# Graph net, second layer: a block's outputs turned in squares by VectorE and through DRAM instead of by TensorE

## Chip, core and metric

One core of one Trainium2 chip runs the whole program in one launch. The metric is the device time in microseconds (us); the time before is the median of three runs. The engines are TensorE (PE in the profile, its weight loads PEld), VectorE (DVE), ScalarE (ACT), GpSimd (POOL) and SyncE (SP, which only issues transfers).

## The reference

Four graph layers on 4096 nodes with 256 features each, every one followed by a residual addition and a normalisation of the rows. All values are FP32. The change lies in the second layer, which is attention with four heads of 64 features, masked by the edges:

```python
def _L1_gnn_ref(x, edge, Wq, bq, Wk, bk, Wv, bv):
    q = _split_heads(x @ Wq + bq)
    k = _split_heads(x @ Wk + bk)
    v = _split_heads(x @ Wv + bv)
    mask = (edge.T.astype(jnp.float32) - 1.0) * 10000.0
    scores = jnp.einsum('hnd,hmd->hnm', q, k) / np.sqrt(HEAD_DIM)
    scores = scores + mask[None, :, :]
    attn = jax.nn.softmax(scores, axis=-1)
    ctx = jnp.einsum('hnm,hmd->hnd', attn, v)
    return ctx.transpose(1, 0, 2).reshape(x.shape[0], NHEAD * HEAD_DIM)
...
x = _layernorm(x + _L1_gnn_ref(x, adj, ...), axis=-1)
```

The first layer is a graph attention with leaky ReLU, the third one with a single head, and the fourth a cosine attention.

## The kernel before

The second layer's main stage works on eight blocks of 512 query rows (`NB`, `b`). A block has 64 steps (`NH`, `j`), one for each 64 keys. A step of a block does the following for all four heads at once, with keys on the partitions and query rows along the free axis:

- `scores` (line 861): eight products on TensorE into a PSUM tile `p` of two banks (L876), and the exponential in place on ScalarE (L878). Every fourth step asks SyncE for the next mask (L869).
- `weights` (line 880): VectorE multiplies by the mask out of PSUM into the SBUF tile `prob` (L888). The sums over the keys are kept in `den`: at even steps GpSimd adds `prob` to it (L898), at odd steps a transfer issued by GpSimd accumulates it (L904). At steps 44, 48, 52 and 56 (`relief`), in all blocks but the first, the even addition is put off and done by VectorE (L1005).
- `sums` (line 906): eight products on TensorE that add the weighted values to the PSUM tiles `acc0` and `acc1` (L912). They run three steps (`LAG`) behind the scores.

The tile `p` has three buffers, `prob` has eight, `acc` one. So the scores of a step need the buffer that VectorE read three steps ago.

At a block's last step the two `acc` tiles, which hold the outputs with features on the partitions and rows along the free axis, are copied to SBUF: `kept0` by ScalarE (L917) and `kept1` by VectorE (L918). The rest of the block, `finish(b, j)` (line 974), is spread over the steps of the next block. Its step `j` is issued in iteration `j + 3` of that next block, as the last thing of the iteration. It joins the key sums (`join_sums`, L921), adds them over the partitions on TensorE and copies them (`row_sums`, L934, L937), turns them on TensorE (`turned_row_sums`, L942), takes reciprocals, turns the outputs on TensorE (`turned_half`, four 128x128 turns for two groups of 128 rows, L949), scales each half in PSUM by the reciprocals (L963), adds it to the rows `X` (L966), and normalises the rows: `one_row` (statistics), `begin_root` (VectorE and ScalarE), `end_root` and `lift_mean` (six small operations on GpSimd, L168 to L191) and `scale_row` (VectorE, L186). The turned pieces take a buffer of `p` through `halves`.

The order on TensorE, VectorE and ScalarE is the order in which the code is written (`manual_schedule`); SyncE and GpSimd get theirs from the scheduler, by the due time of each instruction. The last block has no next block; its `tail` runs beside the third layer's start.

The fourth layer already turns its outputs in another way: VectorE transposes 32x32 squares (L1206), SyncE puts the quarters of the tile to a DRAM tile `away` (L1210) and fetches them back in the right order (L1213).

Of the kernel before, what the change touches and what calls it, by code (L numbers as in the profile page):

```python
# [9 lines left out]
FP = mybir.dt.float32  # L10
# [8 lines left out]
P = 128  # L19
D = 256  # L20
KC = D // P
QB = 4
QW = QB * P
# [5 lines left out]
def kernel(  # L29
# [92 lines left out]
    def turning_apart(squares, far, part, to, eng, between=False):  # L122

        B = P // QB
        squares = squares.tile([P, QB, KC, P], FP, name="squares")
        for c in range(KC):
            if c and between:
                yield
            nc.vector.transpose(squares[:, :, c, :].rearrange("p q (k n) -> p k q n", n=B),
                                part(c).rearrange("p k (q f) -> p k q f", f=B))  # L130
        yield
        far = far.tile([QB, B, QB, KC * P], FP, name="far")
        eng.dma_start(far.rearrange("a f q m -> (a f) (q m)"), squares.rearrange("p q c m -> p (q c m)"))
        yield
        to = to()
        for q in range(QB):
            eng.dma_start(to[q * B:(q + 1) * B], far[:, :, q, :].rearrange("a f m -> f a m"))
        return to.rearrange("p a (c m) -> p c a m", c=KC)

    def block_turning(sb, once, dr, rows, eng):  # L140
        to = lambda: sb.tile([P, KC * QW], FP, name="xT").rearrange("p (a m) -> p a m", a=QB)
        return turning_apart(once, dr, lambda c: rows[:, :, c * P:(c + 1) * P], to, eng)

    def at_once(steps):
        while True:
# [596 lines left out]
    def multi_head_attention(w_sb, b_sb, tail, rows_of_den, rows_done, narrow_edges, ga):  # L742
# [8 lines left out]
        MJ = 4  # L751
        NH = N // d
        W = KC * QW
        kept, den, rden, mvs, roots = {}, {}, {}, {}, {}
        with ExitStack() as lay:
            keep = pool(lay, "mh_keep", 1)
            kT = keep.tile([P, KC, N], FP, name="kT")
            qT = keep.tile([P, KC, N], FP, name="qT")
            V = keep.tile([P, NH, P], FP, name="V")
# [146 lines left out]
            def sums(b, j):  # L906
                if j == 0:
                    acc[b] = [pa.tile([P, QW], FP, name=f"acc{c}") for c in range(KC)]
                for r in range(KC):
                    for c in range(KC):  # L910
                        half = slice(c * d, (c + 1) * d)
                        nc.tensor.matmul(acc[b][c][r * d:(r + 1) * d, :], V[half, j, r * d:(r + 1) * d],  # L912
                                         prob[b, j][half, r, :], start=(j == 0), stop=(j == NH - 1))
                if j == NH - 1:

                    kept[b] = [fin1.tile([P, QW], FP, name=f"kept{c}") for c in range(KC)]
                    nc.scalar.copy(kept[b][0], acc[b][0])  # L917
                    (nc.scalar.copy if b == NB - 1 else nc.vector.tensor_copy)(kept[b][1], acc[b][1])  # L918

            def join_sums(b, n, eng=nc.vector):  # L920
                eng.tensor_tensor(den[b][:, 0, :], den[b][:, 0, :], den[b][:, n, :], OP.add)  # L921
# [1 line left out]
            def row_sums(bank, b):  # L923


                kept[b].append(fin1.tile([P, QW], FP, name=f"kept{KC}"))
                pds = [bank() for _ in range(KC)]
                for r in range(KC):
                    for s in range(2):
                        for c in range(KC):  # L930
                            g = 2 * r + s
                            half = slice(c * d, (c + 1) * d)
                            lo = r * QW + s * QW // 2
                            nc.tensor.matmul(pds[c][g * G:(g + 1) * G, :QW // 2], ones[half, :G],  # L934
                                             den[b][half, 0, lo:lo + QW // 2], start=True, stop=True)
                for c in range(KC):
                    nc.scalar.copy(kept[b][KC][:, c * QW // 2:(c + 1) * QW // 2], pds[c][:, :QW // 2])  # L937

            def turned_row_sums(bank, b):
                pd = bank()  # L940
                for k in range(QB):
                    nc.tensor.transpose(pd[:, k * P:(k + 1) * P], kept[b][KC][:, k * P:(k + 1) * P], ident)  # L942
                return pd

            def turned_half(bank, b, k):
                po = bank().rearrange("p (k f) -> p k f", f=D)
                for i in range(2):
                    for c in range(KC):
                        nc.tensor.transpose(po[:, i, c * P:(c + 1) * P],  # L949
                                            kept[b][c][:, (k + i) * P:(k + i + 1) * P], ident)  # L950
# [17 lines left out]
            def halves():  # L968

                p = ps.tile([P, KC, QW], FP, name="p")  # L970
                left = [p[:, r, :] for r in range(KC)]
                return lambda: left.pop(0)

            def finish(b, j):

                rows = [X[:, b * QB + k, :D] for k in range(QB)]
                if j in (7, 9):
                    join_sums(b, j // 2 - 2)
                elif j == 12:
                    row_sums(halves(), b)  # L980
                elif j == 15:
                    bank = halves()
                    pd = turned_row_sums(bank, b)
                    po = turned_half(bank, b, 0)
                    reciprocals(pd, b)
                    half(po, b, 0)
                elif j == 18:
                    half(turned_half(halves(), b, 2), b, 2)
                elif j in (21, 23, 25, 27):
                    k = (j - 21) // 2  # L990
                    if k == 0:
                        mvs[b] = fin.tile([P, QB, 2], FP, name="mv")
                    one_row(mvs[b], k, rows[k])
                elif j == 29:
                    roots[b] = begin_root(mvs[b])
                elif j == 31:

                    end_root(*roots[b], nc.gpsimd)
                    lift_mean(mvs[b], *roots[b][:2], nc.gpsimd)
                elif j in (35, 37, 39, 41):  # L1000
                    k = (j - 35) // 2
                    scale_row(rows[k], mvs[b], roots[b][1], k)
                if j + LAG - 1 in relief:

                    nc.vector.tensor_tensor(*late.pop(), OP.add)  # L1005
                    ga.dots(b * QB + relief.index(j + LAG - 1), (1,) if b > 1 else (0, 1))
                elif j == 57:
                    ga.factors(b)
                elif j == 59 and b == 0:
                    ga.sources(b)  # L1010
                elif j == 63 and b == 1:
                    ga.row(0, nc.sync)
                elif j == 33 and b == NB - 2:
                    nc.gpsimd.dma_start(ga.first_mask, adjT.rearrange("(t p) i -> p t i", p=P)[:, :QB, :QW])
# [131 lines left out]
    def cosine_attention(co, tail):  # L1146
# [4 lines left out]
        with ExitStack() as lay:  # L1151
# [48 lines left out]

            def squares_far(b, h, both):

                B = P // QB
                sq = fin1.tile([P, QW], FP, name=f"kept{h}").rearrange("p (a k c s) -> p a k c s", a=QB, k=2, c=KC)
                for n, quarter in enumerate(both):
                    nc.vector.transpose(sq[:, :, :, n, :].rearrange("p a k s -> p k a s"),  # L1206
                                        quarter.rearrange("p (k a r) -> p k a r", k=2, r=B))
                away = far.tile([B, QB, QW // P, QB, B], FP, name="away")
                for q in range(QB):
                    nc.sync.dma_start(away[:, :, :, q, :].rearrange("r a m s -> r (a m) s"),  # L1210
                                      sq[q * B:(q + 1) * B].rearrange("r a k c s -> r (a k c) s"))
                t = (fin1 if h else cp).tile([P, QW], FP, name="kept2")
                nc.sync.dma_start(t, away.rearrange("r a m q s -> a r (m q s)"))  # L1213
                back[b, h] = t.rearrange("p (k f) -> p k f", k=2)

            def outputs_far(b, step, seen):
# [241 lines left out]
```

## Time and profile before

| what | value |
| --- | --- |
| median of 3 runs | 2767.89 us (2765.59 to 2771.09) |
| profiled execution, its own time | 2767.82 us |
| profiled execution, span | 2766.0 us |
| granted TensorE clock | 1.0 |
| second layer's main stage | 790.7 to 1692 us |
| TensorE busy | 2750.1 us, 99% |
| VectorE busy | 2311.0 us, 84% |
| ScalarE busy | 1696.6 us, 61% |
| GpSimd busy | 1075.5 us, 39% (none at the start and the end of the span) |
| HBM traffic | 335.94 MB read, 39.40 MB written |

Times in the profile come from one execution and count from the start of its span. A row of a group has the line of the code, the engine, the operation, output and inputs, count, and the durations in ns (minimum, median, maximum); a row of the timeline has start, duration, engine, line, operation, and, in brackets, how long the engine was idle before and what ended that. Rows with the same line may be merged (`x4`, `x8`). Engine names with a `q` are the engine's own queue, which issues transfers and waits.

### The profile page before, as it was taken

The page shows a single profiled execution, that of the slowest core. Times are in us where ns is not written, and L with a number is a line of the kernel's source. Part 1 is how long each engine was busy: PE and PEld are TensorE (multiplying, and loading weights), DVE is VectorE, ACT ScalarE, POOL GpSimd, SP SyncE. Part 2 cuts the span into 40 slices and gives each one's busy share as a digit, 9 for nine tenths or more (in the row PEclk, how much of TensorE's full clock was granted, in tenths as well). Part 3 has the DMA queues.
Part 4 walks back from the last instruction along what each step waited for, and adds up shares of the span by engine and source line. Part 5 has one row for each costly group of instructions (what it writes and reads, how often), then busy time and mean ns, then how long its engine had stood idle before and what let it go on. Part 6 is the DMA issues. An engine that isn't in the chain of part 4 may idle for free. (4 is left out here: it accounts for less than half of the span.)

```text
span 2766.0 us, 50161 instructions
## 1 busy us (share of the span) xinstructions
PE 2750.1 (99%) x19365; PEld 1444.9 (52%) x19365; DVE 2311.0 (84%) x3121; ACT 1696.6 (61%) x2660; POOL 1075.5 (39%) x1020
## 2 busy tenths in 40 slices
PE   9999999999999999999999999999999999999999
PEld 5333333333543333333333336888888777777776
DVE  8899999999777788887888888888888876677776
ACT  8899999999346666666666665565655422222222
POOL 0000000000049878878788786454455000000000
PEclk9999999999999999999999999999999999999999
DMA  8798998987449899898998988577778544454442
GB/s 236 150 191 189 194 196 191 189 188 168 97 117 191 180 190 187 189 190 183 194 187 186 193 178 208 155 203 212 190 197 236 108 76 76 77 81 80 76 70 45
DMA packets 279673, 445.48 MB, mean 161 GB/s; under 512 B 55321, under 2 KB 156169, under 8 KB 274442
## 3 DMA queue, kind: packets, MB, share of 16 engines
q0 software_dynamic: 108784, 216.29, 46.9%
q1 hardware_dynamic: 164280, 218.88, 26.8%
q10 hardware_dynamic: 6370, 7.10, 0.8%
q8 instruction: 152, 2.49, 0.4%
q14 instruction: 87, 0.71, 0.1%
HBM read 335.94 MB, written 39.40 MB: 136 GB/s over the span
## 5 line engine op out<-in xcount | busy, mean ns | idle before, releaser
L888 DVE TENSOR_TENSOR prob<-p,mask 128x1024 f32<-128x1024 f32 x512 | 619.3, 1222 | 162.7 <-ACT p L878 157.0
L878 ACT ACTIVATE p<-p,shift 128x1024 f32<-128x1024 f32 x512 | 555.6, 1088 | 319.7 <-PE p L876 319.1
L338 PE MATMUL acc<-prob,V 128*32 128x512 f32 x5888 | 638.1, 593 | 1.2 <-DVE prob L328 1.1
L898 POOL TENSOR_TENSOR den<-den,prob 128x1024 f32<-128x1024 f32 x220 | 557.6, 2534 | 89.8 <-DVE prob L888 87.1
L313 ACT ACTIVATE prob<-row,dst 128x512 f32<-128x512 f32 x892 | 557.9, 711 | 3.3 <-PE acc L338 2.8
L876 PE MATMUL p<-qT,kT 64*64 64x512 f32 x4096 | 531.5, 591 | 2.3 <-DVE prob L888 2.3
L912 PE MATMUL acc<-prob,V 64*64 64x512 f32 x4096 | 530.1, 589 | 0.0
L328 DVE SCALAR_TENSOR_TENSOR prob<-prob,mask 128x2048 f32<-128x2048 f32 x224 | 507.4, 2285 | 12.6 <-ACT prob L313 11.7
L338 PEld LDWEIGHTS acc<-prob,V 128*32 128x32 f32 x5888 | 189.1, 110 | 434.1 <-issue 407.2
L484 PE MATMUL acc<-mix,mixed 128*128 128x256 f32 x1476 | 401.4, 380 | 1.9 <-DVE quarters L506 1.0
L912 PEld LDWEIGHTS acc<-prob,V 64*64 64x64 f32 x4096 | 157.6, 133 | 281.9 <-issue 280.1
L484 PEld LDWEIGHTS acc<-mix,mixed 128*128 128x128 f32 x1476 | 279.1, 190 | 45.3 <-PE acc L484 3.1
L876 PEld LDWEIGHTS p<-qT,kT 64*64 64x64 f32 x4096 | 154.4, 133 | 279.3 <-issue 252.1
L1185 DVE TENSOR_TENSOR prob<-prob,mask 128x1024 f32<-128x1024 f32 x128 | 156.4, 1222 | 142.9 <-ACT prob L1176 142.9
L904 POOL DMA_DIRECT2D den<-prob x240 | 233.5, 973 | 63.7 <-DMA den<-prob 34.1
L484 PE MATMUL acc<-prob,X 128*128 128x256 f32 x984 | 252.9, 380 | 0.6 <-ACT quarters L498 0.6
L1104 POOL DMA_DIRECT2D mask<-in_adjT x64 | 47.6, 744 | 529.1 <-DVE prob L1185 510.3
L484 PEld LDWEIGHTS acc<-prob,X 128*128 128x128 f32 x984 | 186.8, 190 | 79.8 <-issue 59.2
L617 DVE SCALAR_TENSOR_TENSOR prob<-r,own,mask 128x512 f32<-128x512 f32 x252 | 177.0, 743 | 48.1 <-POOL mix L476 11.9
L1176 ACT ACTIVATE prob<-p 128x512 f32<-128x512 f32 x144 | 86.1, 598 | 212.5 <-PE p L1172 212.5
L325 POOL DMA_DIRECT2D den<-prob x24 | 21.1, 878 | 475.7 <-DVE prob L319 475.7
L1176 ACT ACTIVATE prob<-g 128x512 f32<-128x512 f32 x112 | 66.9, 597 | 199.3 <-PE g L1172 199.3
(245 smaller groups left out, 3044.7 us busy)
## 6 DMA issues: line engine op xcount, KB each, us to landing
mask<-in_adjT SPq DMA_DIRECT2D x254, 512.0 KB
den<-prob POOLq DMA_DIRECT2D x240, 512.0 KB, 5.4
den<-prob POOLq DMA_DIRECT2D x32, 1024.0 KB, 9.2
mask<-edges SPq DMA_DIRECT2D x512, 64.0 KB
mask<-in_adjT POOLq DMA_DIRECT2D x64, 512.0 KB, 5.7
edges<-in_adj POOLq DMA_DIRECT2D x32, 512.0 KB, 17.1
far<-squares SPq DMA_DIRECT2D x16, 512.0 KB
den<-prob SPq DMA_DIRECT2D x16, 512.0 KB
```

The lines of the kernel that those rows point to most:

```text
L313: seen = nc.scalar.activation(z[:, h, :], r, AF.Relu, bias=-1.0, scale=dst[:, j, h:h + 1])
L328: nc.vector.scalar_tensor_tensor(z, z, 1.0, mask[m][:, j % MJ, :].unsqueeze(1).to_broadcast([P, H, QW]), OP.add, OP.mult)
L338: nc.tensor.matmul(acc[b][h * G:(h + 1) * G, n, :], part, prob[b, j][:, h, :], start=(j == 0), stop=(j == NT - 1 and n < HC))
L484: nc.tensor.matmul(acc[at][:, half * HW:(half + 1) * HW], w, a, start=(g == 0 and n in (0, 2, 3, 5)), stop=(g == NP - 1), skip_group_check ...
L617: nc.vector.scalar_tensor_tensor(z[:, n, :], r, ga.own[:, j:j + 1], mask[:, n, :], OP.add, OP.mult)
L876: nc.tensor.matmul(p[c * d:(c + 1) * d, r, :], kT[half, c, at:at + d], qT[half, c, cols], start=True, stop=True)
L878: nc.scalar.activation(p, p, AF.Exp, bias=shift)
L888: nc.vector.tensor_tensor(z, p, mask[m][:, j % MJ, :].unsqueeze(1).to_broadcast([P, KC, QW]), OP.mult)
L898: nc.gpsimd.tensor_tensor(to, to, flat, OP.add)
L904: nc.gpsimd.dma_start(to, flat, accum_op=OP.add)
L912: nc.tensor.matmul(acc[b][c][r * d:(r + 1) * d, :], V[half, j, r * d:(r + 1) * d], prob[b, j][half, r, :], start=(j == 0), stop=(j == NH - 1))
L1185: nc.vector.tensor_tensor(z, z, co.mask[b, 2 * g // MJ][:, lo:lo + 2, :], OP.mult)
```

## The change

In the second layer, for all blocks but the last, the outputs are no longer turned by TensorE. VectorE transposes the 32x32 squares of the two `acc` tiles with four instructions of 128x256: two out of PSUM at the block's last step (in the place of the copy to `kept1`), and one each in finish steps 1 and 2, from `kept0`. ScalarE issues eight transfers of 64 KB (`put_quarter`, runs of 128 bytes) to a DRAM tile, one at every other finish step from 4 to 18, and two of 256 KB that fetch them back into SBUF (`fetch`, steps 15 and 23). A half is then scaled and added from SBUF, not from PSUM. Row sums move from step 12 to 13, their turn and the reciprocals to 17, the halves from 15 and 18 to 22 and 29, the statistics of the rows from 21, 23, 25, 27 to 24, 26, 30, 32, the root from 29 and 31 to 34 and 36, and the scaling of the rows from 35, 37, 39, 41 to 39, 40, 41, 43. On GpSimd, the six small root operations stood between the addition of step 32 and the transfer of step 33; they now stand between the transfer of step 37 and the addition of step 38. The fourth layer uses the same helpers as before under new names, and its order of instructions is the same.

```diff
+    def squares_of(t):
+        return t.rearrange("p (a k c s) -> p a k c s", a=QB, k=2, c=KC)
+    def turn_squares(sq, n, quarter):
+        nc.vector.transpose(sq[:, :, :, n, :].rearrange("p a k s -> p k a s"),
+                            quarter.rearrange("p (k a r) -> p k a r", k=2, r=P // QB))
+    def put_quarter(away, sq, q, eng=nc.sync):
+        B = P // QB
+        eng.dma_start(away[:, :, :, q, :].rearrange("r a m s -> r (a m) s"),
+                      sq[q * B:(q + 1) * B].rearrange("r a k c s -> r (a k c) s"))
+    def fetch(t, away, eng=nc.sync):
+        eng.dma_start(t, away.rearrange("r a m q s -> a r (m q s)"))
...
+            far = pool(lay, "mh_turned", 1, space=bass.MemoryType.DRAM)
...
                 if j == NH - 1:
-                    kept[b] = [fin1.tile([P, QW], FP, name=f"kept{c}") for c in range(KC)]
+                    if b == NB - 1:
+                        kept[b] = [fin1.tile([P, QW], FP, name=f"kept{c}") for c in range(KC)]
+                        for c in range(KC):
+                            nc.scalar.copy(kept[b][c], acc[b][c])
+                        return
+                    kept[b] = [fin1.tile([P, QW], FP, name="kept0")]
                     nc.scalar.copy(kept[b][0], acc[b][0])
-                    (nc.scalar.copy if b == NB - 1 else nc.vector.tensor_copy)(kept[b][1], acc[b][1])
+                    squares[b] = [squares_of(fin1.tile([P, QW], FP, name=f"kept{1 + h}")) for h in range(2)]
+                    for h in range(2):
+                        turn_squares(squares[b][h], 1, acc[b][1][:, h * HW:(h + 1) * HW])
...
             def finish(b, j):
-                if j in (7, 9):
+                if j in (1, 2):
+                    h = j - 1
+                    turn_squares(squares[b][h], 0, kept[b][0][:, h * HW:(h + 1) * HW])
+                    back[b, h] = far.tile([P // QB, QB, QW // P, QB, P // QB], FP, name=f"away{h}")
+                elif j in range(4, 20, 2):
+                    h, q = divmod((j - 4) // 2, QB)
+                    put_quarter(back[b, h], squares[b][h], q, nc.scalar)
+                elif j in (15, 23):
+                    h = (j - 15) // 8
+                    t = fin1.tile([P, QW], FP, name=f"kept{1 + h}")
+                    fetch(t, back[b, h], nc.scalar)
+                    back[b, h] = t.rearrange("p (k f) -> p k f", f=D)
+                elif j in (7, 9):
                     join_sums(b, j // 2 - 2)
-                elif j == 12:
+                elif j == 13:
                     row_sums(halves(), b)
-                elif j == 15:
-                    bank = halves()
-                    pd = turned_row_sums(bank, b)
-                    po = turned_half(bank, b, 0)
-                    reciprocals(pd, b)
-                    half(po, b, 0)
-                elif j == 18:
-                    half(turned_half(halves(), b, 2), b, 2)
-                elif j in (21, 23, 25, 27):
+                elif j == 17:
+                    reciprocals(turned_row_sums(halves(), b), b)
+                elif j in (22, 29):
+                    half(back.pop((b, (j - 22) // 7)), b, (j - 22) // 7 * 2)
+                elif j in (24, 26, 30, 32):
...
-                elif j == 29:
+                elif j == 34:
                     roots[b] = begin_root(mvs[b])
-                elif j == 31:
+                elif j == 36:
                     end_root(*roots[b], nc.gpsimd)
                     lift_mean(mvs[b], *roots[b][:2], nc.gpsimd)
-                elif j in (35, 37, 39, 41):
+                elif j in (39, 40, 41, 43):
```

More of the change, by code (lines that the diff above doesn't have):

```diff
@@ L142, in block_turning, with put_far @@
         return turning_apart(once, dr, lambda c: rows[:, :, c * P:(c + 1) * P], to, eng)
+    def squares_of(t):
[7 more added lines that the diff above has]
+                      sq[q * B:(q + 1) * B].rearrange("r a k c s -> r (a k c) s"))
+    def put_far(far, sq):
+        B = P // QB
+        away = far.tile([B, QB, QW // P, QB, B], FP, name="away")
+        for q in range(QB):
+            put_quarter(away, sq, q)
+        return away
+    def fetch(t, away, eng=nc.sync):
+        eng.dma_start(t, away.rearrange("r a m q s -> a r (m q s)"))
     def at_once(steps):
@@ L753, in multi_head_attention @@
         W = KC * QW
-        kept, den, rden, mvs, roots = {}, {}, {}, {}, {}
+        HW = QW // 2
+        kept, den, rden, mvs, roots, squares, back = {}, {}, {}, {}, {}, {}, {}
         with ExitStack() as lay:
             keep = pool(lay, "mh_keep", 1)
+            far = pool(lay, "mh_turned", 1, space=bass.MemoryType.DRAM)
             kT = keep.tile([P, KC, N], FP, name="kT")
@@ L923, in row_sums @@
             def row_sums(bank, b):
-                kept[b].append(fin1.tile([P, QW], FP, name=f"kept{KC}"))
+                total = kept[b, "den"] = fin1.tile([P, QW], FP, name=f"kept{0 if b < NB - 1 else KC}")
                 pds = [bank() for _ in range(KC)]
@@ L936, in row_sums @@
                 for c in range(KC):
-                    nc.scalar.copy(kept[b][KC][:, c * QW // 2:(c + 1) * QW // 2], pds[c][:, :QW // 2])
+                    nc.scalar.copy(total[:, c * QW // 2:(c + 1) * QW // 2], pds[c][:, :QW // 2])
             def turned_row_sums(bank, b):
@@ L941, in turned_row_sums @@
                 for k in range(QB):
-                    nc.tensor.transpose(pd[:, k * P:(k + 1) * P], kept[b][KC][:, k * P:(k + 1) * P], ident)
+                    nc.tensor.transpose(pd[:, k * P:(k + 1) * P], kept[b, "den"][:, k * P:(k + 1) * P], ident)
                 return pd
@@ L976, in finish @@
                 rows = [X[:, b * QB + k, :D] for k in range(QB)]
-                if j in (7, 9):
+                if j in (1, 2):
[11 more added lines that the diff above has]
+                elif j in (7, 9):
                     join_sums(b, j // 2 - 2)
-                elif j == 12:
+                elif j == 13:
                     row_sums(halves(), b)
-                elif j == 15:
-                    bank = halves()
-                    pd = turned_row_sums(bank, b)
-                    po = turned_half(bank, b, 0)
-                    reciprocals(pd, b)
-                    half(po, b, 0)
-                elif j == 18:
-                    half(turned_half(halves(), b, 2), b, 2)
-                elif j in (21, 23, 25, 27):
-                    k = (j - 21) // 2
+                elif j == 17:
[3 more added lines that the diff above has]
+                elif j in (24, 26, 30, 32):
+                    k = (24, 26, 30, 32).index(j)
                     if k == 0:
@@ L993, in finish @@
                     one_row(mvs[b], k, rows[k])
-                elif j == 29:
+                elif j == 34:
                     roots[b] = begin_root(mvs[b])
-                elif j == 31:
+                elif j == 36:
                     end_root(*roots[b], nc.gpsimd)
                     lift_mean(mvs[b], *roots[b][:2], nc.gpsimd)
-                elif j in (35, 37, 39, 41):
-                    k = (j - 35) // 2
+                elif j in (39, 40, 41, 43):
+                    k = (39, 40, 41, 43).index(j)
                     scale_row(rows[k], mvs[b], roots[b][1], k)
@@ L1201, in squares_far @@
             def squares_far(b, h, both):
-                B = P // QB
-                sq = fin1.tile([P, QW], FP, name=f"kept{h}").rearrange("p (a k c s) -> p a k c s", a=QB, k=2, c=KC)
+                sq = squares_of(fin1.tile([P, QW], FP, name=f"kept{h}"))
                 for n, quarter in enumerate(both):
[L1206 to L1211, printed above, removed]
+                    turn_squares(sq, n, quarter)
                 t = (fin1 if h else cp).tile([P, QW], FP, name="kept2")
-                nc.sync.dma_start(t, away.rearrange("r a m q s -> a r (m q s)"))
+                fetch(t, put_far(far, sq))
                 back[b, h] = t.rearrange("p (k f) -> p k f", k=2)
```

## Prediction

> **What bounds the kernel now.** I read the page first: busy shares, then the stretches of the second layer's stage, then the order of single instructions inside one finishing step. The shares (part 1 of the page):
>
> ```profile
> PE 2750.1 (99%) x19365; PEld 1444.9 (52%) x19365; DVE 2311.0 (84%) x3121; ACT 1696.6 (61%) x2660; POOL 1075.5 (39%) x1020
> ```
>
> TensorE is the bound, so a TensorE instruction taken out is time taken out, if nothing else becomes late. Next, the windows of three blocks (third, fourth, fifth; columns: stretch, length, busy PE, PEld, DVE, ACT, POOL, clock, DMA share, GB/s):
>
> ```profile
> 1011.60:1126.42 114.82, 112.93 (x1056) 40.38 (x1052) 97.86 (x108) 71.24 (x72) 91.46 (x66) 1.00 0.95 186
> 1126.42:1238.98 112.56, 112.56 (x1057) 40.50 (x1052) 92.16 (x100) 71.22 (x72) 92.18 (x66) 1.00 0.90 188
> 1238.98:1351.53 112.55, 112.55 (x1056) 40.49 (x1052) 92.14 (x100) 71.21 (x72) 92.32 (x66) 1.00 0.90 188
> ```
>
> PE is busy 112.55 of 112.55 us: nothing waits. But DVE (92.1, 82%), POOL (92.3, 82%) and DMA (0.90) have little to spare. The third block lost 1.9 us (114.82 less 112.93). Now what a turn costs (PE's timeline, fifth block):
>
> ```profile
> 1271.49 1.04 PE L912 MATMUL acc<-prob,V 64*64 64x512 f32 x8
> 1272.46 0.66 PE L942 MATMUL p<-ident,kept 128*128 128x128 f32 x4
> 1272.95 0.60 PE L949 MATMUL p<-ident,kept 128*128 128x128 f32 x4
> 1273.48 1.09 PE L876 MATMUL p<-qT,kT 64*64 64x512 f32 x8
> 1274.39 1.04 PE L912 MATMUL acc<-prob,V 64*64 64x512 f32 x8
> 1275.25 1.04 PE L876 MATMUL p<-qT,kT 64*64 64x512 f32 x8
> ...
> 1277.83 1.04 PE L912 MATMUL acc<-prob,V 64*64 64x512 f32 x8
> 1278.79 0.66 PE L949 MATMUL p<-ident,kept 128*128 128x128 f32 x4
> 1279.38 1.09 PE L876 MATMUL p<-qT,kT 64*64 64x512 f32 x8
> ```
>
> A group of L876 or L912 starts every 0.86 us (1274.39 to 1275.25), so a step is 1.717. With row sums and first half turned together, the step at 1271.49 has 1.99 to the next scores, 1.13 too much; with the second half alone 1.55, 0.69 too much, and each sequence costs about 0.05 more in the group behind it (1273.48 to 1274.39 is 0.91).
>
> **Removed from PE.** Row sums alone will cost what the second half costs alone, 0.74. So a block goes from 1.18 + 0.74 to 0.74: 1.18 us saved. Seven blocks: 8.3 us. The last block is unchanged.
>
> **How late VectorE may be.** The scores of 1268.91 are multiplied by the mask at 1271.14 (1.22 long, the next instruction can start 1.14 after it), ending at 1272.36; their PSUM bank, one of three, is wanted again three steps later, 1268.91 + 5.15 = 1274.06. VectorE may be 1.70 us late before PE waits, and each step has 1.717 - 1.14 = 0.58 to catch up.
>
> **Added on VectorE, cheap.** Four square turns of 0.44 per block (median of the same instruction in the fourth layer), two of them instead of a copy of 0.68 (L918): +0.20 at the hand-over, +0.44 in each of two later steps, under the 0.58. Nothing. The last block's copy and the other stages keep their order: nothing.
>
> **Moved, and the port.** This is the term that decides. L898 is GpSimd's addition. At 1032 us a VectorE addition of two SBUF operands met it (timeline, third block):
>
> ```profile
> 1031.66 2.94 POOL L898 TENSOR_TENSOR den<-den,prob 128x1024 f32<-128x1024 f32 x1
> 1032.21 3.48 DVE L921 TENSOR_TENSOR den<-den 128x1024 f32<-128x1024 f32 x1
> ...
> 1036.88 1.09 PE L876 MATMUL p<-qT,kT 64*64 64x512 f32 x8 [1.06 <-DVE prob L888]
> ```
>
> L921 takes 1.215 at the median; here it takes 3.48, ending one L921 after the addition, and PE idles. The operations of a half are not touched today, since one operand comes from PSUM:
>
> ```profile
> L966 DVE TENSOR_TENSOR X<-p,X x14: 691/691/692, 935.2 to 1618.7; 128x512 f32<-128x512 f32 x14
> L186 DVE TENSOR_SCALAR X<-X,mv,r x68: 399/408/1826, 190.4 to 2163.0; 128x256 f32<-128x256 f32 x68
> ```
>
> Fourteen times within 1 ns; L186, all in SBUF, spreads to 1826. After the change both operations of each half read two SBUF operands, and fall into L921's class. The Trainium skill ("SBUF — State Buffer", section "Who interferes with whom") says the same and speaks against the change: a VectorE instruction with two SBUF inputs contends with a GpSimd instruction that reads SBUF, an exclusive lock, the first to issue blocks the other fully. By the rule every half that meets an addition waits for all of it; by the L966 row as it stands, none would.
>
> Finish step j runs in iteration j+3, after that iteration's mask product; additions follow the product of even iterations, median 2.354 us, 0.15 after it ends.
> - First half, j=22, iteration 25 (odd): the addition of 24 ends 0.15 + 2.35 - 1.72 = 0.8 after product 25; then 0.69 + 0.69. The next product is late by 0.08 + 0.8 + 1.38 - 0.58 = 1.7: just covered, 0.
> - Second half, j=29, iteration 32 (even): its multiplication starts first, the addition queues, and I take it that it gets in between the two operations. From the product's start: 1.14 + 0.69 + 2.35 + 0.69 = 4.87, against 1.72: late 3.15, PE waits 3.15 - 1.70 = 1.45. Bounds: 0 (VectorE keeps the port for both) and 1.45.
> - Scale rows, j=39, 40, 41, 43, where before they stood at 35, 37, 39, 41, each behind an even product. The one in iteration 43 meets the addition of 42: blocked about 1.0, next product late by 0.9. Iteration 44 (no addition) leaves 0.8, and iteration 45 has the relief addition and a dot (L1005 1.215, L552 0.42; 1.55 by spacing): late 1.9, PE waits 0.2. In the first two blocks two dots, so 0.6 here and 0.3 at the next relief step: 0.9. Bounds 0 and 0.9.
> - GpSimd's six small root operations (0.19 to 0.20 each, L168 to L191; 1.65 in all by spacing) now stand before the addition of iteration 38 instead of before the transfer of 33. That addition waits for a product which is itself behind ScalarE's root; between 0 and 0.3, taken as 0.
>
> **Added on ScalarE's queue.** Eight puts and two fetches per block. The same puts on SyncE:
>
> ```profile
> L1210 SPq DMA_DIRECT2D away<-kept x56: 550/630/2049, 2230.6 to 2694.8; - x56
> 1270.02 1.09 ACT L878 ACTIVATE p<-p,shift 128x1024 f32<-128x1024 f32 x1 [0.63 <-PE p L876]
> ```
>
> An issue is 0.55 to 0.63 when not in a burst; ScalarE idles 0.63 before each exponential, and one issue comes every other step. Behind it waits the next exponential, behind that the product and PE: even 1.2 long, 0.6 late is inside 1.70. Nothing. A fetch (j=15, 23) is queued five steps, 8.6 us, after its last put; SyncE's waits at the same place in layer four lasted at most 8.0. On time. Iteration 16, with the row-sum copies, has no put. SyncE's queue is the same list as before. GpSimd's only passed item is the root.
>
> **Added on the DMA queues.** From the window 2230:2250, which holds eight puts and two fetches:
>
> ```profile
> q1 hardware_dynamic: 4485, 1.05, 24.9%
> ```
>
> 24.9% of 20 us is 5.0 us of all engines per block, 4.4% on 0.90, wanted within 20 steps; in such a stretch (1253.3 to 1286.9) the share is 0.88, which leaves 4.0. The block's share becomes 0.945, the third block's 0.95. Price between 0 and that block's 1.9; its loss began with a late transfer wait, so nearer to 0: I take 0.3.
>
> **Sum.** Five blocks: -1.18 + 1.45 + 0.2 + 0.3 = +0.77. First two: -1.18 + 1.45 + 0.9 + 0.3 = +1.47. Together 3.85 + 2.94 = +6.8. The profiled execution took 2767.82 (span 2766.0), 0.07 under the median of the three runs: 2774.6. About 0.2%, 5.5 us, is what a measurement of this kernel can tell from no change, so this is slower, barely.
>
> **Rivals.**
> - *VectorE keeps the port* (faster). If the second operation of the half at iteration 32 issues without a gap, the queued addition stays out and its 1.45 is 0. For it: L963 and L966 follow each other today at 0.69 spacing. Against it: 1032 us shows no order between two. With 0.3 for DMA: five blocks -0.68, two 0.0: -3.4, 2764.4; without the DMA term 2762.3, and with the relief steps covered too, -8.3, 2759.5. It decides at 1.18 - 0.5 = 0.7 of PE wait per block.
> - *ScalarE is held by a fetch* (much slower). If puts land later than 8.6 + 1.7 + 0.6 = 10.9 us, exponentials stop. Landing at 12 costs 1.1 twice per block, 15 us: with +6.8 about 2790, without the half's wait 2780. For it: DMA 0.95 and small packets. Against it: 8.0 as the longest wait.
> - *Turning is hidden anyway*, that is, PE takes out no time: excluded by PE's 112.55 of 112.55.
>
> **How the numbers follow.** Forecast 0.45 (same 0.14, slower 0.31, as the half's wait moves between 0.9 and 1.6); VectorE keeps the port 0.35 (faster 0.22, as either small term at 0 takes it under 2762.4, same 0.13); ScalarE or transfers held 0.15, slower; the rest 0.05, faster 0.03, slower 0.02. Faster 0.25, same 0.27, slower 0.48. The range leaves out the ends of the first and third: 2759.5, less a little for a third block without its stall, 2759, to 2788.
>
> **What would show it.** PE: 56 L949 rows fewer, and the row-sum turn at about 0.74. Half operations of 0.69 behind odd products stretched to 1.5, and in iteration 32 the second stretched to 3. PE waits on a VectorE tile around iterations 35 and 48. Put issues near 0.56, fetch waits none. The forecast is wrong if half operations keep 0.69 throughout, if PE's waits name ScalarE, or if blocks take under 111.9.

## The result: 1.3% slower

The changed kernel took 2805.82 us (median of 4, 2803.26 to 2808.42) against 2768.95 for the kernel before in the same comparison: ratio 1.0134, 95% interval 1.0120 to 1.0148. The forecast of 2774.6 had the direction; the loss (36.9 us, forecast 6.8) is more than five times as large, and the time lies outside the range. The profiled execution, the slowest of the four, has a span of 2806.6 us, 40.6 more than before; the second layer's stage, from the first scores to the last, accounts for 39.9 of them (896.9 to 936.8).

The busy shares of the changed kernel:

```profile
PE 2754.4 (98%) x19309; PEld 1448.9 (52%) x19309; DVE 2367.3 (84%) x3142; ACT 1696.1 (60%) x2660; POOL 1076.8 (38%) x1020
```

56 TensorE instructions are gone; VectorE is 56 us busier. The windows of the third, fourth and fifth block (columns as before):

```profile
1017.43:1139.47 122.04, 114.18 (x1048) 40.85 (x1044) 105.81 (x111) 71.16 (x72) 91.79 (x66) 0.99 0.93 184
1139.47:1258.37 118.90, 113.77 (x1049) 41.51 (x1045) 101.19 (x103) 71.13 (x72) 92.56 (x66) 0.99 0.91 187
1258.37:1376.52 118.15, 113.79 (x1049) 41.73 (x1044) 100.36 (x103) 71.12 (x72) 92.71 (x66) 0.99 0.91 188
```

TensorE now waits some 5 us in a block, VectorE is 8 to 9 us busier, and the DMA share hardly moves. VectorE's groups (line, instruction, count: minimum/median/maximum ns, first and last start) show where its time went:

```profile
L995 DVE TENSOR_TENSOR kept<-kept,rden x14: 681/1914/3496, 946.7 to 1674.1; 128x512 f32<-128x512 f32 x14
L998 DVE TENSOR_TENSOR X<-kept,X x14: 691/3171/3389, 950.3 to 1675.9; 128x512 f32<-128x512 f32 x14
L205 DVE TENSOR_SCALAR v<-mv x31: 151/163/1698, 182.3 to 2778.9; 128x4 f32<-128x4 f32 x31
```

The operations of the halves (L963 and L966 before, 0.69 each) take 0.68 to 3.50, about three times as long on average, and `v`, the tiny first step of the root (0.16), up to 1.70. The timeline of the sixth block shows how (rows between those shown are left out):

```profile
1420.32 0.87 POOL L929 DMA_DIRECT2D den<-prob  x1 [2.67 <-DMA den<-prob]
1420.93 2.66 POOL L923 TENSOR_TENSOR den<-den,prob 128x1024 f32<-128x1024 f32 x1
...
1423.95 2.86 POOL L923 TENSOR_TENSOR den<-den,prob 128x1024 f32<-128x1024 f32 x1
...
1424.34 3.02 DVE L995 TENSOR_TENSOR kept<-kept,rden 128x512 f32<-128x512 f32 x1
1427.40 0.69 DVE L998 TENSOR_TENSOR X<-kept,X 128x512 f32<-128x512 f32 x1
1429.28 1.09 PE L901 MATMUL p<-qT,kT 64*64 64x512 f32 x8 [1.26 <-DVE prob L913]
...
1437.91 1.87 DVE L995 TENSOR_TENSOR kept<-kept,rden 128x512 f32<-128x512 f32 x1
1439.80 2.64 POOL L923 TENSOR_TENSOR den<-den,prob 128x1024 f32<-128x1024 f32 x1
1439.81 3.19 DVE L998 TENSOR_TENSOR X<-kept,X 128x512 f32<-128x512 f32 x1
1444.19 1.09 PE L901 MATMUL p<-qT,kT 64*64 64x512 f32 x8 [2.66 <-DVE prob L913]
...
1448.96 2.55 POOL L923 TENSOR_TENSOR den<-den,prob 128x1024 f32<-128x1024 f32 x1
1449.86 1.70 DVE L205 TENSOR_SCALAR v<-mv 128x4 f32<-128x4 f32 x1
1451.65 0.20 ACT L184 ACTIVATE r<-v 128x4 f32<-128x4 f32 x1 [3.50 <-DVE v L205]
...
1451.99 3.08 ACT L903 ACTIVATE p<-p,shift 128x1024 f32<-128x1024 f32 x3
1453.17 4.78 DVE L913 TENSOR_TENSOR prob<-p,mask 128x1024 f32<-128x1024 f32 x4 [1.61 <-POOL s L193]
...
1454.45 1.09 PE L901 MATMUL p<-qT,kT 64*64 64x512 f32 x8 [1.44 <-DVE prob L913]
```

Three scenes. First half: GpSimd waits 2.67 for an earlier accumulating transfer, so its additions come late, and L995 ends 0.5 after the one that began at 1423.95. Second half: L995 waits for a late addition, then the next addition (1439.80) gets in before L998 (1439.81), which ends 0.5 after it. Root: `v` ends when the addition ends; ScalarE's root has waited 3.50, the exponentials queued behind it run in a row, and the mask products and TensorE follow (the releaser named at 1453.17 is merely the latest event; the product waited for its exponential).

In what follows, a wait "at step n" is the time by which the scores of step n+1 start later than 1.717 after those of step n. "Block" is the mean distance of the block starts over the fourth to seventh block. In the second to seventh block of the changed kernel the waits are 1.4 to 2.3 at step 28 (first half), 2.5 to 4.1 at step 35 (second half), and 0.45 at 48, 0.9 in the first two (scale rows and relief). The root's 1.6 at step 40 stands in the second and the sixth block only. In the third, fourth, fifth and seventh, 1.5 to 1.75 stand at steps 36 and 37, ahead of `v`, and there it is the granted clock. The windows of the sixth and the seventh block, 3.4 us of each behind the second half's wait, and TensorE's lines of the seventh:

```profile
1376.52:1494.49 117.97, 112.33 (x1048) 41.17 (x1044) 101.14 (x103) 71.13 (x72) 92.47 (x65) 1.00 0.91 188
1494.49:1612.94 118.45, 113.79 (x1048) 41.73 (x1044) 100.53 (x103) 71.14 (x72) 92.43 (x65) 0.99 0.90 188
1444.20:1447.60 3.40, 3.40 (x32) 1.21 (x36) 3.24 (x7) 1.62 (x2) 2.51 (x2) 1.00 0.60 113
1562.80:1566.20 3.40, 3.40 (x20) 1.06 (x20) 3.24 (x7) 1.09 (x1) 2.65 (x2) 0.50 0.62 117
```

```profile
1562.65 1.87 PE L901 MATMUL p<-qT,kT 64*64 64x512 f32 x8 [2.94 <-DVE prob L913]
1564.28 1.95 PE L937 MATMUL acc<-prob,V 64*64 64x512 f32 x8
1565.98 1.17 PE L901 MATMUL p<-qT,kT 64*64 64x512 f32 x8
```

After TensorE's wait of 2.94 the granted clock is 0.50, a group takes 1.87 where the sixth block's takes 1.09, and the next scores start 1.6 late. The trace has one such stretch of 3.41 us in each of these four blocks, behind waits of 2.6 to 3.9, and none in the sixth, whose wait was 2.66; so no threshold can be read from it. TensorE's busy time is 113.8 in such blocks and 112.3 in the sixth, though both have the same work.

### The profile page after: what moved, and what is told of

Read it like the earlier page. It is cut to its first block, busy times and chain, and to the rows that moved or that the text cites. A ratio compares the mean times of both kernels' runs of the same rounds, so it can differ in the third digit from the quotient of the medians.

```text
span 2806.6 us, 50190 instructions
## 1 busy us (share of the span) xinstructions
PE 2754.4 (98%) x19309; PEld 1448.9 (52%) x19309; DVE 2367.3 (84%) x3142; ACT 1696.1 (60%) x2660; POOL 1076.8 (38%) x1020
## 5 line engine op out<-in xcount | busy, mean ns | idle before, releaser
L901 PE MATMUL p<-qT,kT 64*64 64x512 f32 x4096 | 539.2, 595 | 38.0 <-DVE prob L913 38.0
L937 PE MATMUL acc<-prob,V 64*64 64x512 f32 x4096 | 536.6, 592 | 0.0
L937 PEld LDWEIGHTS acc<-prob,V 64*64 64x64 f32 x4096 | 164.5, 134 | 278.7 <-issue 277.9
```

Of the source, the lines that this page charges most:

```text
L901: nc.tensor.matmul(p[c * d:(c + 1) * d, r, :], kT[half, c, at:at + d], qT[half, c, cols], start=True, stop=True)
```

## The experiments

| kernel | ratio to before (95%) | block, us |
| --- | --- | --- |
| before | 1 | 112.55 |
| changed | 1.0134 (1.0120 to 1.0148) | 118.37 |
| e1 halves from PSUM | 1.0116 (1.0099 to 1.0133) | 115.86 |
| e2 no transfers | 1.0068 (1.0053 to 1.0083) | 115.41 |
| e3 before, halves in SBUF | 1.0009 (1.0000 to 1.0018) | 113.20 |
| e4 two additions fewer on GpSimd | 1.0096 (1.0080 to 1.0112) | 116.53 |
| e5 root one step later | 1.0162 (1.0146 to 1.0179) | 118.69 |
| e6 long runs | 1.0073 (1.0054 to 1.0091) | 115.66 |
| e7 no transfers, places changed | 1.0035 (1.0022 to 1.0048) | 113.97 |
| e8 no halves, places changed | 1.0082 (1.0066 to 1.0097) | 116.04 |
| e9 eight additions more on VectorE | 1.0100 (1.0087 to 1.0113) | 116.37 |
| e10 before, six additions more on VectorE | 1.0023 (1.0014 to 1.0032) | 113.17 |
| e11 additions of even steps 20 to 42 left out | 0.9986 (0.9975 to 0.9998) | 112.16 |
| e12 runs of 512 bytes into DRAM | 1.0082 (1.0065 to 1.0099) | 115.41 |
| e13 e12, second half odd | 1.0062 (1.0046 to 1.0078) | 114.49 |
| e14 e13, v and scale rows even | 1.0018 (1.0009 to 1.0028) | 112.81 |
| e15 e14, scale rows later | 1.0021 (1.0012 to 1.0030) | 112.90 |
| e16 second half parted | 1.0038 (1.0026 to 1.0050) | 113.53 |
| e17 e16, scale rows earlier | 1.0035 (1.0023 to 1.0047) | 113.34 |

**e1, is it the port?**

```diff
-                    half(back.pop(...), b, ...)
+                    po = halves()()
+                    nc.tensor.matmul(po, ident, flat, start=True, stop=True)   # flat: the fetched half
+                    half(po.rearrange("p (k f) -> p k f", f=D), b, ...)
```

> The changed kernel, but each fetched half is first copied to PSUM by TensorE (one 128x512 product with the identity, about 0.74 us on the path), and VectorE scales and adds it from there; the transfers, squares and steps stay. PORT theory (VectorE's half operations, with two SBUF operands, wait for whole GpSimd additions): all half operations at 0.69 again, PE's waits of 1.4 to 2.3 at step 28 and 2.5 to 4.1 at step 35 gone, two copies paid per block: 2806 - 7 x (1.65 + 2.8) + 7 x 1.45 = about 2785, and less (about 2775) if the waits at steps 36 to 48 were left-over lateness. TRANSFER theory (puts and fetches delay the accumulating transfers, GpSimd and so VectorE): nothing gained, 2806 + 10 = 2816.

```profile
L995 DVE TENSOR_TENSOR p<-p,rden x14: 689/690/699, 945.9 to 1662.4; 128x512 f32<-128x512 f32 x14
L998 DVE TENSOR_TENSOR X<-p,X x14: 691/692/693, 946.6 to 1663.2; 128x512 f32<-128x512 f32 x14
```

With one operand in PSUM the same operations, at the same steps and with the same transfers, never wait, and the waits at 28 and 35 are gone, as is the lowered clock. The root's 1.1 to 2.0 at step 40 and 0.46 at 48 are left. The whole time still went to neither forecast. Two reasons: a copy costs 1.17 on TensorE's path, not 0.74, so 2.3 per block are given back (block 115.86); and the stage, 10.1 us shorter than in the changed kernel, is followed by layers that took 9.6 us longer. In the trace TensorE waits there 4.3 for a transfer (`xT<-far`, at 1923 us), the clock is 0.5 for 3.4 us behind it, and 1.3 are lost at 2153 us. That this comes of e1's edit is not shown: e10, which has none of the change, waits for the same tile, 4.1 at the longest.

**e2, how much are the transfers?**

```diff
-                    put_quarter(...)  /  fetch(...)
+                    # none: half() reads the tiles of squares
```

> The changed kernel without the eight puts and two fetches of a block: the halves are read from the SBUF tiles of squares where they stand (the transposition of the outputs is left incomplete). PORT: still slow, the second half blocked as now; the first one less if GpSimd is no longer late behind its transfer waits: 2790 to 2806. TRANSFER: the half operations back near 0.69 to 1.5, blocks at 111.4 to 112, time 2760 to 2765.

```profile
L997 DVE TENSOR_TENSOR kept<-kept,rden x14: 750/876/1482, 946.7 to 1653.9; 128x512 f32<-128x512 f32 x14
L1000 DVE TENSOR_TENSOR X<-kept,X x14: 691/3174/3373, 948.2 to 1654.7; 128x512 f32<-128x512 f32 x14
```

Half the loss. The first half costs nothing outside the third block (no wait at 28), the second 1.73 at step 35: the first of its operations is short and the second takes 3.17, an addition of 2.35 and its own 0.69. The root's wait stands at step 40 in all seven blocks (1.57 to 1.64), 0.46 at 48, and the clock keeps 1.00 in the whole stage. The transfers' part, with all that follows from them, is 118.37 - 115.41 = 3.0 per block.

**e3, one part alone.** The kernel before with `half(kept[b][0 or 1])` in place of `half(turned_half(...))`, so that the outputs stay unturned.

> The kernel before with one part of the change alone: both half operations read two SBUF operands (the copied outputs as they are; the turn of the outputs by TensorE is left out), at the old steps 15 and 18, no squares, no transfers. PORT: each half is blocked for an addition or more: half operations mean over 1.5 us, 1.5 to 5 us lost per block less 1.2 saved, 2770 to 2795. TRANSFER: PE saves 1.2 per block and nothing is lost: 2760.

The two operations of a half take 1.5 and 1.8 on average, TensorE waits 0.75 at step 21 and 0.85 at 24, and the 1.14 saved is more than used up: block 113.2. So the operands alone cost 1.6 to 1.8 per block at those steps.

**e4, additions out of the way.**

```diff
+            spare = (24, 32)   # added by VectorE one iteration later
-                elif j in (22, 29):
+                elif j in (21, 29):
-                elif j in (39, 40, 41, 43):
+                elif j in (41, 45, 49, 53):
```

> The changed kernel with its transfers, but GpSimd leaves out the additions of steps 24 and 32 in all blocks but the first (VectorE makes them one iteration later, as it does at 44 to 56), the first half goes to finish step 21, so that both halves stand in iterations without an addition, and the four scale rows go to steps 41, 45, 49, 53, also in iterations without one. PORT: halves at 0.69 or with one short wait behind a late addition of step 22 or 30, PE's waits mostly gone: 2760 to 2772. TRANSFER: the waits stay where GpSimd is late: 2790 or more.

A miss. The scale rows fell from a mean of 0.96 to 0.41 and the wait at 48 went, but L995 still took 2.0: with the transfers in place GpSimd was late by more than the two additions gave it. VectorE's own two additions cost 0.55 each (steps 28 and 36), and the root's wait, 1.8 at step 40, now stood in every block, with the clock at 1.00.

**e5 to e8, what the rest is.** e5: `begin_root` at step 35, `end_root` at 37.

> The changed kernel with the start of the root moved by one step, from 34 to 35 (iteration 38, even, as in the kernel before) and its end from 36 to 37. PARITY theory: at an odd iteration the small VectorE operation v (0.16 us) waits for the running addition, ScalarE's root waits for v, and the next exponential waits behind the root; at an even iteration v goes first. Then v is back at 0.16, PE's wait of 1.6 at steps 36 or 40 goes: 7 x 1.6 = 11 us less, ratio to before about 1.0095 instead of 1.0134. Rival LATENESS: that wait is only what the halves left over, and the time stays (1.013).

A miss too. In the second and the sixth block, where the root's wait had stood at 40, it went, and 1.3 came back at step 46, where the scale rows (mean 1.11) met the additions. In the third, fourth, fifth and seventh block 1.7 stayed at steps 36 and 37: that is the lowered clock, 0.5 for 3.41 us in the same four blocks, and no place of the root could remove it. e6: the puts and fetches at their steps, but DRAM written and read in runs of 2 KB (the halves then hold other values).

> The changed kernel with the same transfers and bytes in runs of 2 KB (each put writes 32 partitions as they stand, each fetch reads them back: the rows come back in another order, so the halves hold other values). SHORT RUNS: the 128-byte packets cost the accumulating transfers their time; with long runs the transfers' part, about 3.0 us per block (118.4 less 115.4 without transfers), goes: 2806 - 21 = 2785, ratio 1.006. VOLUME: any transfer of that volume does it, ratio 1.013.

As without transfers. e7 is e2 with the root of e5 and the scale rows of e4:

> No transfers (halves read from the squares, as in e2), the root at steps 35 and 37, the scale rows at 41, 45, 49, 53 (iterations without an addition). PORT and PARITY: of the waits of e2 only the second half's 1.7 per block is left: block 112.55 - 1.1 + 1.7 = 113.2, ratio 1.002. Rival LATENESS: the waits at 40 and 48 stay, ratio 1.006.

There the wait at 40 does go (`v` at 0.45, block 113.7 in three of the four; 1.73 at 35 and 0.48 at 48 are left, and 0.90 at 52 in one). So the root's place decides once GpSimd is not late. e8 is the changed kernel with those places and without the halves:

> The changed kernel with all transfers and squares, but the four operations of the two halves are left out (the outputs are never added), the root at 35 and 37, the scale rows at 41, 45, 49, 53. PORT: the transfers alone do no harm, nothing of VectorE is late: block 112.55 - 1.1 = 111.4, ratio 0.997. TRANSFER: the waits behind late accumulations stay, block over 113, ratio over 1.002.

A miss that shows the transfers' way. GpSimd's and VectorE's lines (fifth block):

```profile
1309.62 0.87 POOL L929 DMA_DIRECT2D den<-prob  x1 [3.02 <-DMA den<-prob]
...
1335.07 1.23 DVE L1045 TENSOR_TENSOR den<-den,prob 128x1024 f32<-128x1024 f32 x1 [1.96 <-POOL den L923]
```

GpSimd waits 3 us for an accumulation, has some 0.25 idle in two steps to catch up with, and is still late at the relief step, where VectorE's own addition must follow GpSimd's. Without the halves, the bill is only paid later: 2.6 to 3.0 at step 48 in three of the four blocks, with the clock at 0.5 behind it (1.45 to 1.7 at step 49), and 2.2 at step 41 in the other.

How late GpSimd is, by the time from the end of an odd step's mask product to the issue of its accumulation (sixth block, us):

| step | 17 | 19 | 21 | 23 | 25 | 27 |
| --- | --- | --- | --- | --- | --- | --- |
| before | 0.8 | 0.3 | 0.8 | 0.8 | 0.8 | 0.8 |
| changed | 0.4 | 0.7 | 2.8 | 2.3 | 2.1 | 1.3 |
| e2 no transfers | 0.3 | 0.8 | 0.3 | 0.8 | 0.8 | 1.3 |
| e6 runs of 2 KB | 0.3 | 0.8 | 0.6 | 0.8 | 0.8 | 1.3 |
| e12 runs of 512 bytes | 0.3 | 0.8 | 0.3 | 0.8 | 1.1 | 1.3 |

The transfers themselves show it too. The accumulation of step 17 lands 9.3 to 10.2 us after its issue in the changed kernel, 4.6 to 5.4 before, 5.1 to 6.1 in e2, 6.6 to 8.2 in e6 and 5.5 to 6.8 in e12. In the changed kernel those of steps 19, 23 and 25 are late as well (6.7 to 9.6), those of steps 9 and 13, which have puts but no fetch beside them, hardly (5.2 to 6.7).

**e9 to e11, GpSimd's load.** e9: `spare = (12, 16, 20, ..., 40)`, halves at 21 and 29, root at 33, scale rows as in e4.

> The changed kernel with its transfers, and in all blocks but the first VectorE also makes the additions of steps 12, 16, 20, 24, 28, 32, 36 and 40, one iteration later, so that GpSimd has 2.35 us free in every four steps. Halves at 21 and 29, the root's start at 33 and the scale rows at 41, 45, 49, 53: all in iterations without an addition. NO SLACK ON GPSIMD (transfers make GpSimd late, it can't catch up, and VectorE pays at the port and where its own addition follows GpSimd's): waits mostly gone, block 111.5 to 112.3, ratio 0.997 to 1.001. Rival VECTORE FULL: eight more additions of 1.14 per block make VectorE late by themselves, ratio 1.005 or more.

e10, the control on the kernel before: `spare = (12, 16, 24, 28, 32, 40)`.

> The kernel before, with VectorE making the additions of steps 12, 16, 24, 28, 32 and 40 as well, one iteration later. A control for the one above: VectorE has 0.58 free per step, so nothing should become late: block 112.55, ratio 1.000 (0.999 if the third block's 1.9 goes). VECTORE FULL: ratio over 1.003.

e11: the additions of steps 20 to 42 left out.

> The changed kernel at its own steps, but in all blocks but the first GpSimd's additions of the even steps 20 to 42 are left out altogether (the row sums lack them). Transfers, puts on ScalarE and the order of VectorE's operations stay. NO SLACK ON GPSIMD: nothing meets the halves, v and the scale rows: half operations at 0.69, v at 0.16, PE's waits at 28, 35, 36 and 40 gone, 0.5 to 0.9 left at 48; block about 112, ratio 0.998 to 1.000. Rival TRANSFERS OR SCALARE DIRECTLY: the waits stay, ratio over 1.005.

e9 missed: L998 at 0.69, `v` at 0.16 and the scale rows at 0.41 show that nothing gets in between any more, but L995 (mean 2.4) still waits for the late addition of step 22 or 30. The rival came true beside it: VectorE's additions cost 0.55 at steps 28, 36 and 40 in e9, and 0.6 per block at step 15 in the control. e11 settles whether GpSimd's additions are what the halves, `v` and the scale rows wait for. Its groups, and the window of a block:

```profile
L997 DVE TENSOR_TENSOR kept<-kept,rden x14: 681/682/692, 946.8 to 1637.1; 128x512 f32<-128x512 f32 x14
L1000 DVE TENSOR_TENSOR X<-kept,X x14: 691/692/694, 947.5 to 1637.8; 128x512 f32<-128x512 f32 x14
L205 DVE TENSOR_SCALAR v<-mv x31: 151/161/209, 182.4 to 2748.5; 128x4 f32<-128x4 f32 x31
```

```profile
1354.44:1465.85 111.41, 111.41 (x1048) 41.58 (x1044) 92.32 (x103) 71.22 (x72) 65.30 (x54) 1.00 0.98 202
```

With puts, fetches and VectorE's order as in the changed kernel, TensorE is busy without a gap and the block takes 111.41, 1.14 less than before: the whole gain, no wait, and the DMA share at 0.98. So it is in three of the four blocks. In the fifth GpSimd, which still waits for late accumulations (4.2 at 1326 us), holds up VectorE's relief addition, and TensorE waits 2.98 at step 52; hence the mean of 112.16 (the profiled execution, 2778, is the slowest of ten with a median of 2767.6). So late accumulations alone do no harm until an engine has to wait for GpSimd.

**e12, which packets.** The turn's short runs moved from the write to DRAM to the way back.

```diff
-                eng.dma_start(away[:, :, :, q, :]..., sq[q * B:(q + 1) * B]...)          # DRAM in runs of 128 bytes
+                nc.scalar.dma_start(away[q].rearrange("a r f -> r a f"), sq[q * B:(q + 1) * B]...)   # 512 bytes
-                eng.dma_start(t, away.rearrange("r a m q s -> a r (m q s)"))
+                nc.scalar.dma_start(t.rearrange("p (m q s) -> p m q s", ...)[:, :, q, :], away[q]...)  # one per q
```

> The changed kernel with the order of the turn done on the way back: eight puts of a block write DRAM in runs of 512 bytes (2048 bytes in e6, 128 in the changed kernel), and eight fetches of 64 KB read DRAM in one piece and write SBUF in runs of 128 bytes; sixteen issues on ScalarE instead of ten, the halves and all later steps as in the changed kernel. SHORT WRITES TO DRAM are what holds the accumulating transfers: GpSimd no longer late at steps 21 to 25, wait at 28 gone, ratio about 1.007 as with long runs. SHORT PACKETS of any kind: as now or worse, ratio 1.013 or more.

The same outputs, as many packets of 128 bytes in the other direction, more packets in all (5376 instead of 4488 in the fifth block's stretch) and 16 issues instead of 10: and GpSimd is in time, with block and waits as in e2 (1.73, 1.63, 0.45). e6 keeps the steps and the fetches of 256 KB, e12 the short packets; what both take away is the writes of 128 bytes to DRAM, so the accumulations are not held without them. Whether such writes do it alone, or only with a large fetch behind them, is not shown: the late accumulations are those in flight with a fetch.

**e13 to e17, by place alone.** All keep every transfer and operation of e12. e13: second half at 28.

> The kernel of e12 with the second half moved by one step, from 29 to 28, that is from iteration 32 (even) to 31 (odd), where it waits once for what is left of the addition of iteration 30 and no addition can get in between its two operations. MEETING THEORY: the wait of 1.73 at step 35 goes as the first half's did, the waits at 40 and 48 stay: block 115.4 - 1.7 = 113.7, ratio about 1.004. LATENESS (any four operations on two SBUF operands cost so much): block 115.4, ratio 1.008.

e14: also root at 33 and 34, last statistics at 31, scale rows at 39, 41, 45, 49.

> e13 with the start of the root at step 33 (iteration 36, even), its end at 34, the last statistics at 31 and the scale rows at 39, 41, 45, 49 (iterations 42, 44, 48, 52, all even). MEETING THEORY: v at 0.16, the wait at 40 gone, at 48 0 to 0.5: block 111.4 to 112.0, ratio 0.997 to 1.000, so no longer slower than before. LATENESS: the waits only move: block over 113, ratio over 1.003.

e15: scale rows at 41, 45, 49, 53.

> e14 with the scale rows at 41, 45, 49, 53 (iterations 44, 48, 52, 56, in which GpSimd adds nothing). MEETING THEORY: as e14 or 0.1 to 0.4 per block better: block 111.4 to 111.9, ratio 0.996 to 0.999. LATENESS: over 1.003.

The wait of the second half fell from 1.73 to 0.95 (e13), that of the root from 1.46 to 0 and that at 48 to 0.3 (e14). e14's groups:

```profile
L995 DVE TENSOR_TENSOR kept<-kept,rden 128x512 f32<-128x512 f32 x14 | 28.6, 2043 | 0.0
L998 DVE TENSOR_TENSOR X<-kept,X 128x512 f32<-128x512 f32 x14 | 9.7, 692 | 0.5
L205 DVE TENSOR_SCALAR v<-mv 128x4 f32<-128x4 f32 x8 | 1.7, 214 | 0.0
```

(busy us and mean ns after the bar). At odd iterations the first operation waits once, the second never; `v` goes first. The block comes from 118.4 to 112.8, but not under 112.55, so e14 and e15 missed their forecast; and of the 6.3 us that e14's stage is still longer than before, 4.3 lie in the second and third block. e16 parts the second half over steps 26 and 28, and e17 also has the scale rows at 37, 41, 45, 49:

> The kernel of e15 with the two operations of the second half in two steps, 26 and 28 (iterations 29 and 31, both odd), and the second statistics at 25. MEETING THEORY: each waits at most for what is left of one addition, 0.8 to 1.3, and is caught up before the next; the wait of 0.95 at step 34 goes, if the fetch has landed: block 111.8, ratio 0.999 to 1.000. FLOOR: it moves to step 32 or 34, block 112.8, ratio 1.002.

> e16 with the scale rows at 37, 41, 45, 49 (iterations 40, 44, 48, 52). MEETING THEORY: as e16, and the 0.32 at step 48 is less, since nothing but the relief addition is left near it: ratio 0.998 to 1.000. FLOOR: as e16.

Missed as well: the wait only split, 0.42 at step 32 and 0.71 at 34. The kernel before stays the fastest of the kernels that compute everything.

## Why the prediction was wrong, point by point

- *Removed from PE, 1.18 per block.* Right: 1.14 (e11).
- *Squares on VectorE, nothing.* Right: no trace has a wait at steps 1 to 5 that the kernel before does not have.
- *ScalarE's queue, nothing.* Right, and the rival that a fetch holds it fell:

```profile
L154 ACTq DMA_DIRECT2D away<-kept x56: 556/557/666, 912.1 to 1651.6; - x56
ACT p L903 <- DMA away<-kept: 1.6, 1, 1.6
```

An issue takes 0.56 as predicted, and one exponential in the whole stage waited for a put (second line, from the list of waits: us in total, times, longest).
- *First half 0, second half 1.45.* Right in kind where GpSimd is in time: 0 and 1.73 without transfers, the second mis-sized by 0.28. The rival "VectorE keeps the port" fell: a queued addition gets in between two operations that stood at 0.69 spacing before. The Trainium skill's rule ("SBUF — State Buffer", "Who interferes with whom") holds in e1, with one operand in PSUM, and in e11, without additions: all 28 operations take 0.68 to 0.70.
- *Scale rows 0.2 (0.9 in the first two blocks).* 0.46 and 0.92 at step 48 without transfers: a term mis-sized by 0.26 in five blocks.
- *The root, taken as 0.* This step failed. It followed GpSimd's six operations past its queue, but not `v`, which the change moves from iteration 32 to 37, from even to odd. `v` has all its operands in SBUF like the scale rows, meets the addition, and holds ScalarE's root and the exponentials behind it: 1.63 per block, 11 us, without transfers (e2). e7 and e14, with `v` at an even iteration, do not have this wait. In the changed kernel itself it stood in two of the seven blocks; in four the lowered clock stood in its place. The rule that I had applied to halves and scale rows should have been put to every VectorE instruction that the diff moves.
- *Transfers 0.3 per block.* This step failed most: 3.0 per block, or 19.7 us of the stage (936.8 against 917.1 in e2). The working asked whether the DMA engines have time left (share 0.90 to 0.945). They had; the measured share was 0.91, and e11 runs three blocks at 111.41 with 0.98 in the one shown. What mattered was how late each accumulation lands, since GpSimd waits for it in its own queue and has no time to catch up, and the form of the packets: with 128-byte writes to DRAM the accumulations come late, with the same bytes in 512-byte or 2-KB runs little or not at all. The Trainium skill ("DMA: Bandwidth & Descriptors", "Specifications") names 512 bytes as the least for line rate, with a read-modify-write below. For writes to DRAM e6 and e12 agree with that, though nothing between 128 and 512 bytes was run; e12's packets of 128 bytes into SBUF are below it too and cost nothing measurable (block 115.41 with them and without any transfer). Nothing here shows the mechanism.
- *The granted clock, not in the sum.* The forecast let TensorE run at full clock behind any wait. In four of the seven blocks it ran at 0.5 for 3.41 us, 6.5 us in all; e2 has none of it in the stage, nor have e6, e7 and e12 to e17, so it is counted in the transfers' 3.0.

The terms together, per ordinary block: -1.14 + 1.73 + 1.63 + 0.46 gives 2.7 (e2 measured 2.9), and 3.0 more for the transfers is 5.7; measured 118.37 - 112.55 = 5.8. The transfers' 3.0 are, by the waits of the fourth to seventh block, 1.5 at step 28, 1.4 more at step 35 and 1.2 of lowered clock, less 1.2 because the root's wait stood in only one of the four. The forecast had -1.18 + 1.45 + 0.2 + 0.3.

Open: why accumulations land late beside short writes, and when the clock falls. The 0.95 that e14 keeps at step 34 can be followed in its sixth block: the addition beside L995 began 1.42 before it in the first half, which took 1.48, and 0.89 before it in the second, which took 2.54; GpSimd, set back by the first half, had no idle time in front of that addition.

## What to carry to other kernels

Where two engines lock each other out, list every instruction that a change moves or whose operands it moves, tiny ones too, and ask at which point of the other engine's rhythm each will be issued: here an operation that went first cost nothing, one that came second cost the rest of the other's, and a pair let the other in between. GpSimd, with 3.2 us of work in every 3.4 (an addition of 2.35 and an issue of 0.87 in two steps), could not absorb a late transfer; its lateness was carried on until something had to wait for it. Judge added transfers by what lands later, not by the share of busy time, and try long writes to DRAM, with the short runs of a layout change on the way back: here that was worth 3.0 us per block. Before a wait is put down to an engine, look at the granted clock of the same stretch.

## What the runs showed of the hardware that was not expected

- 256 KB per half through DRAM with 128-byte writes delayed accumulations of 512 KB on another queue (that of step 17 landed in 9.3 to 10.2 us, 4.6 to 5.4 before), and GpSimd waited up to 3.2 us for them; with 512-byte writes and 128-byte runs into SBUF it took 5.5 to 6.8, at a higher count of packets.
- The granted clock fell to 0.5 for 3.41 us behind TensorE waits of 2.6 to 3.9 us in four blocks, 1.5 to 1.75 us each, and did not behind one of 2.66.
- A 128x512 product with the identity costs 1.17 us of TensorE's path, four 128x128 turns of the same data 0.69 to 0.74.
- A 128x4 operation of 0.16 us on VectorE took 1.70 beside an addition on GpSimd (2.81 at the most, in e8).
